# Layer 1 attention of a two-layer kernel: residual, last bias and attention's sum added by DVE instead of by identity products on PE, with a new planning order

## The chip, the cores and the metric

The kernel runs on one core of a Trainium2 chip. Five engines work in parallel, each through its own queue in order: PE (matrix products, with a separate weight-load row PEld), DVE (vector), ACT (scalar and activation functions), POOL (which here issues the scatters) and SP (which issues most of the loads). The metric is the device time of one execution in microseconds (us), given as the median of several runs. A profile is one further execution; it has its own time.

## The reference, cut to what matters

Two layers, each an attention part and a mixture-of-experts part, on eight batches of 512 tokens with 128 channels. The change lies in layer 1's attention:

```
x  = x + o.reshape(Bb, Tt, HEADS * DV) @ Wo
h2 = _ln(x, ln_w, ln_b)
return x + jax.nn.gelu(h2 @ W1 + b1, approximate=False) @ W2 + b2
```

This is applied to `_layernorm(x)` of the stream, and the stream itself is added outside: `x = x + _L1_attn_ref(_layernorm(x), ...)`. So four things meet in the stream that the router of layer 1's experts then reads: the stream before the attention, the attention's sum (with its own residual), the output of the GELU part, and the bias `b2`. `o` comes from a gated linear recurrence over the tokens, which the kernel runs as a scan.

## The kernel before, in words

The tokens of a batch lie as a tile of 128 partitions x 4 x 128 (one PSUM bank). Each batch is one "block". Layer 0's attention and experts come first and end near 440 us. Then the stage around the change begins: for each of the eight blocks a coroutine `attend(b)` and, behind it, `route1(b, px)`. After that stage the routed rows are read back expert by expert (`fetch`, `first`, `second`, lines 1698 to 1775), and the results are gathered and added (line 1825).

The order within the stage is not written by hand. Each coroutine yields the engine that it needs next and a cost, and a planner (`Order.run`) picks, of all the blocks' next steps, the one that can start first by those costs; ties and ranks are settled by the lists TURN, TURN_REST and TURN_ROUTE, one number for each block. What the planner picks becomes the fixed order of every engine's queue. A changed cost or rank therefore changes the order of all five queues.

The steps of a block that matter below:

- line 1162: `ys`, layer 0's expert results, is loaded; line 1174: PE adds the stream `x_b` and both halves of `ys` into a PSUM tile `px` by products with the identity; lines 1148 and 1149: DVE takes the moments.
- lines 450 and 456: ACT normalises `px` into `hn`; PE transposes it (line 440), and products with the weights follow (1234, 1250, 1263, 1275), with ACT functions behind them.
- line 1190, `residual()`: ACT copies `px` into `x_b`, gives the PSUM tile back, and normalises `x_b` into `u`, the attention's input.
- lines 1241 and 1299: ACT's queue writes keys, queries and decays to DRAM; line 1223: SP reads them back spread over the partitions as `kb`, `gb_both`, `qb_both`, 1 MB each.
- lines 1306, 1313, 1317: DVE's product, scan and product over 128 x 2048 elements. Line 1327: PE sums the result. Lines 1344, 1349, 456, 1337, 1355: the gated root-mean-square norm.
- lines 1360 and 1362: PE adds `u` (identity) and the product with `Wo` into a PSUM tile `pu`; moments, normalisation, transposes, line 1394 (W1), line 1398 (GELU, into `mT`).
- line 1377, `keep_sum()`: ACT copies `pu` back into `u`.
- line 1405: PE adds `x_b`, the bias `b2` and `u` into a new PSUM tile with three identity products of 128 x 512; line 1409: eight products with W2 go on top. `b2` lies on all partitions.
- `route1`: moments, normalisation, transposes, router product (1445), the eight best and their numbers on DVE (1457 to 1464), counts (1485 to 1489), their sums over the partitions on PE (1493, 1494), the target rows `si` (1502), ACT's copies of the row and its weight into one of six `rows` buffers (1552, 1553), and for each of 128 pairs of token tile and choice one scatter on POOL (line 1540). Each group of four scatters has a numbering instruction before it (1535). The expert stage can begin only when all 128 have landed.

The four PSUM tiles named `acc` (line 1085) are shared by 1174, 1327, 1360 and 1405.

Of the kernel before, what the change touches and what calls it, by code (L numbers as in the profile page):

```python
# [63 lines left out]
PE, DVE, ACT, POOL, SP = "PE", "DVE", "ACT", "POOL", "SP"  # L64
# [125 lines left out]
def two_layers(ctx: ExitStack, tc: tile.TileContext, a: dict, out: bass.AP):  # L190
    nc = tc.nc
# [9 lines left out]
    def ring(pool, n, shape, name, dtype=F32):  # L201
        return Ring([pool.tile(shape, dtype, tag=f"{name}{i}", bufs=1, name=f"{name}{i}") for i in range(n)])
# [6 lines left out]
    def load(name, shape, src, queue=nc.gpsimd, pool=const):  # L209
        t = pool.tile(shape, F32, name=name)  # L210
        queue.dma_start(t, src)
        return t

    xs = []
    for b in range(B):
        x_b = keep.tile([P, NT, C], F32, tag="x", name=f"x_{b}")
# [8 lines left out]
    ident = const.tile([P, P], F32, name="ident")  # L225
# [68 lines left out]
    tokens, columns = [P, NT, C], [P, S]  # L294
# [60 lines left out]
    b2 = load("b2", [P, C], a["L1_attn_b2"].partition_broadcast(P))  # L355
# [6 lines left out]
    order = Order()  # L362
# [79 lines left out]
    def tiled(t2):  # L442
        return t2.rearrange("p (t c) -> p t c", t=NT)

    def chunk(t2, t):
        return t2[:, t * P : (t + 1) * P]

    def affine(dst, src, rs, sh):
        for t in range(NT):
            nc.scalar.activation(  # L450
                dst[:, t, :], src[:, t, :], AF.Identity, bias=sh[:, t : t + 1], scale=rs[:, t : t + 1]
            )
# [6 lines left out]
    def landing(us):  # L459
        s = Signal()  # L460
        s.set(order.later(us))
        return s
# [595 lines left out]
    u_ring = ring(work, 4, tokens, "u")  # L1058
# [26 lines left out]
    acc_ring = ring(stage_psum, 4, columns, "acc")  # L1085
    FLIGHT = 5

    TURN = [-56.5, 2.5, 31.0, 55.5, 10.0, 34.5, 86.0, 12.5]
    TURN_REST = [-12.5, -2.5, -24.0, 28.5, -84.0, 41.5, 163.0, 24.5]
    TURN_ROUTE = [-34.0, -91.5, -74.0, 17.0, -71.0, 58.5, 11.5, 42.5]  # L1090

    class Small:

# [41 lines left out]
    order = Order()  # L1135
# [21 lines left out]
    def attend(b):  # L1157

        x_b = xs[b]
# [9 lines left out]
        m = yield flight  # L1169
        yield landed  # L1170
        px = yield acc_ring
# [13 lines left out]
        u = yield u_ring  # L1185
        have_u = Signal()

        def residual():
            yield ACT, 0.6
            nc.scalar.copy(x_b, tiled(px))  # L1190
            acc_ring.give(order.now, px)
            yield ACT, 1.65
            affine(u, x_b, m.rs["u"][:, 0, :], m.sh["u"][:, 0, :])
            have_u.set(order.now)

        hn = yield hn_ring
        yield ACT, 1.65
        affine(hn, tiled(px), m.rs["u"][:, 1, :], m.sh["u"][:, 1, :])
        order.add(TURN[b], residual())
        ps = yield bank_ring  # L1200
        yield PE, 0.65
# [10 lines left out]
        def used_hT():  # L1212
            uses[0] -= 1
            if uses[0] == 0:
                h1_ring.give(order.now, hT)
# [15 lines left out]
        def keys_queries():  # L1231
# [11 lines left out]
            yield landing(LANDING)  # L1243
            order.add(TURN[b], spread_rows(pairs[b][:ng], kb_ring, have_kb, Signal()))
            order.add(TURN[b], spread_rows(pairs[b][ng:], qb_ring, have_qb, Signal(), gb_issued))

# [26 lines left out]
        ps = yield bank_ring  # L1273
        yield PE, 0.98
        nc.tensor.matmul(ps[:ng, :], lhsT=gkw, rhs=hT, start=True, stop=True)
        used_hT()
        order.add(TURN[b], keys_queries())
        order.add(TURN[b], values())
        order.add(TURN[b], gating())

# [9 lines left out]
        ps = yield bank_ring  # L1290
# [29 lines left out]
        if finished[0] == B:  # L1320
            all_scanned.set(order.now)
        yield Rank(TURN_REST[b])

# [21 lines left out]
        squared.set(order.now)  # L1345
        order.add(TURN_REST[b], gated())
        ps = yield bank_ring
# [10 lines left out]
        pu = yield acc_ring  # L1358
        yield PE, 2.1
        nc.tensor.matmul(tiled(pu), lhsT=ident, rhs=u, start=True, stop=False)  # L1360
        for t in range(NT):
            nc.tensor.matmul(chunk(pu, t), lhsT=chunk(yT, t), rhs=wo1, start=False, stop=t == NT - 1)
        y_ring.give(order.now, yT)
        yield DVE, 1.5
        moments(m, tiled(pu), "m")
        yield ACT, 0.4, EXP
# [6 lines left out]
        have_sum = Signal()  # L1373

        def keep_sum():
            yield ACT, 0.6
            nc.scalar.copy(u, tiled(pu))
            acc_ring.give(order.now, pu)
            have_sum.set(order.now)

        order.add(TURN_REST[b], keep_sum())
        ps = yield bank_ring
        yield PE, 0.65
# [16 lines left out]

        yield have_sum
        ps = yield acc_ring
        yield PE, 5.0
        for part in (x_b, b2.unsqueeze(1).to_broadcast(tokens), u):
            nc.tensor.matmul(tiled(ps), lhsT=ident, rhs=part, start=part is x_b, stop=False)
        for t in range(NT):
            out_t = chunk(ps, t)
            for c in range(2):
                nc.tensor.matmul(
                    out_t,  # L1410
                    lhsT=mT[:, c, t * P : (t + 1) * P],
                    rhs=w2[:, c, :],
                    start=False,
                    stop=t == NT - 1 and c == 1,
                )
        m_ring.give(order.now, mT)
        u_ring.give(order.now, u)
        flight.give(order.now, m)
        order.add(TURN_ROUTE[b], route1(b, ps))

    def route1(b, px):
# [59 lines left out]

        order.add(TURN_ROUTE[b], shares())

# [45 lines left out]

        order.add(TURN_ROUTE[b], biases())  # L1530
        sent = [Signal() for _ in range(NT)]
# [17 lines left out]
        for t in range(NT):  # L1549
# [3 lines left out]
            nc.scalar.copy(rw[:, :, WEIGHT], m.ex[:, t, :])  # L1553
            order.add(TURN_ROUTE[b], scatter(t, rw))
        xr_ring.give(order.now, xr)
# [308 lines left out]
```

## Time and profile before

| what | value |
|---|---|
| median of 3 runs (lowest, highest) | 994.44 us (993.44, 996.89) |
| the profiled execution's own time | 989.84 us |
| its span, first to last instruction | 988.1 us |
| mean granted PE clock | 0.865 |
| PE busy | 786.4 us (80%) |
| DVE busy | 615.4 us (62%) |
| ACT busy | 490.4 us (50%) |
| POOL busy | 447.9 us (45%) |
| line 1405, three forms, 16 matmul rows each | 10.1, 10.0 and 9.0 us busy |
| line 1190, ACT copy of `px` | 8 times, median 596 ns |
| line 1377, ACT copy of `pu` | 8 times, median 620 ns |
| line 1540, scatters on POOL | 128 times, median 964 ns, 556.6 to 757.7 us |

Busy time is how long an engine's instructions ran; its share of the span is a mean over stages with different limits. A product of 128 x 512 in fp32 stands as two matmul rows in the profile, so eight products are 16 rows. The rows of pipelined products overlap, so what a product costs the engine is the distance from its start to the next one's start, not its duration. The granted clock says what part of full speed PE had.

### The profile page before, as it was taken

Reading aid. Unit: us, or ns where it says so; the run is one execution under the profiler, and the core shown is the slowest. Engines: PE = TensorE matmul, PEld = TensorE weight load, DVE = VectorE, ACT = ScalarE, POOL = GpSimd, SP = SyncE. Lnnn points to the kernel's source line nnn. Section 1 sums busy time; section 2 is a strip of 40 time slices with the busy share of each in tenths; the row PEclk is TensorE's granted clock in tenths of the full one; section 3 lists DMA queues with packets and bytes.
Section 4 is the critical chain, followed back from the end, with each engine's and each line's share of the span. In section 5 each row is a group of like instructions: output and inputs, shape, how many; then the busy total and the mean of one; then the engine's idle time right before and its main releaser. Section 6 shows DMA issues by size and latency. Waiting matters only on the chain. (4 is left out here: it accounts for less than half of the span.)

```text
span 988.1 us, 12411 instructions
## 1 busy us (share of the span) xinstructions
PE 786.4 (80%) x3523; PEld 487.0 (49%) x3523; DVE 615.4 (62%) x1599; ACT 490.4 (50%) x1072; POOL 447.9 (45%) x469
## 2 busy tenths in 40 slices
PE   5988899899598889977779999969755999888500
PEld 3634466455254544433224544435432999778500
DVE  5579998879769411112478568686442787666408
ACT  5644665565253403435766988756620555444200
POOL 7200002330845361550000378587775577777750
PEclk9888889799977889998898998979757999999955
DMA  7897674739324503004995067777112544332139
GB/s 174 213 261 160 162 187 107 197 96 215 79 71 109 164 8 86 23 22 148 221 238 137 33 153 203 172 182 212 52 49 66 129 126 116 108 104 81 54 115 348
DMA packets 75527, 132.91 MB, mean 135 GB/s; under 512 B 12819, under 2 KB 54673, under 8 KB 67265
## 3 DMA queue, kind: packets, MB, share of 16 engines
q1 hardware_dynamic: 46400, 91.12, 36.6%
q0 software_dynamic: 14832, 28.88, 9.8%
q10 hardware_dynamic: 14224, 12.11, 4.3%
q8 instruction: 28, 0.46, 0.2%
q14 instruction: 43, 0.34, 0.1%
HBM read 94.79 MB, written 41.14 MB: 138 GB/s over the span
## 5 line engine op out<-in xcount | busy, mean ns | idle before, releaser
L1540 POOL DMA_INDIRECT rows<-rows,si x128 | 148.9, 1164 | 159.6 <-issue 140.9
L880 POOL DMA_INDIRECT row<-rows,si x64 | 90.6, 1415 | 211.3 <-DVE qT L591 109.1
L1775 POOL DMA_INDIRECT res<-qy,to x144 | 139.9, 971 | 57.8 <-issue 29.2
L1744 ACT ACTIVATE qh<-mid,qw 128x128 f32<-128x128 f32 x288 | 79.7, 377 | 116.8 <-PE mid L1738 81.5
L675 PE MATMUL acc<-add,center 128*128 128x512 f32 x128 | 78.6, 770 | 17.3 <-DVE add L704 14.7
L1738 PE MATMUL mid<-dT,qw 128*128 128x128 f32 x576 | 74.7, 282 | 15.9 <-DVE dT L1728 15.9
L1738 PEld LDWEIGHTS mid<-dT,qw 128*128 128x128 f32 x576 | 68.9, 195 | 21.1 <-DVE dT L1728 21.0
L1756 PE MATMUL qyp<-qw,qh 128*128 128x128 f32 x576 | 71.7, 277 | 0.0
L698 DVE TENSOR_TENSOR_SCAN add<-dec,add 128x2048 f32<-128x2048 f32 x16 | 70.8, 4424 | 0.7
L1756 PEld LDWEIGHTS qyp<-qw,qh 128*128 128x128 f32 x576 | 68.3, 194 | 0.0
L179 ACT ACT_TABLE_LOAD x48 | 61.6, 1283 | 5.8 <-issue 3.2
L675 PEld LDWEIGHTS acc<-add,center 128*128 128x128 f32 x128 | 30.7, 251 | 62.4 <-issue 35.3
L1016 POOL DMA_INDIRECT res<-y,de x32 | 31.5, 984 | 43.3 <-DVE y L1010 35.7
L1712 DVE COPY qw<-fw 128x258 f32 x144 | 45.7, 317 | 8.5 <-ACT qh L1744 1.4
L666 ACT ACTIVATE dec<-dec 128x2048 f32<-128x2048 f32 x16 | 30.5, 1908 | 30.0 <-DVE dec L686 30.0
L1327 PE MATMUL acc<-kb,ident 128*128 128x512 f32 x64 | 36.1, 716 | 10.1 <-DVE kb L1317 10.1
L1713 DVE COPY qw<-fw 128x256 f32 x144 | 43.1, 300 | 0.2 <-issue 0.2
L793 PE MATMUL bank<-xT,rw 128*128 128x512 f32 x64 | 38.5, 733 | 5.3 <-ACT xT L785 3.6
L1148 DVE BATCH_NORM_STATS2 st<-acc 128x6 f32<-128x128 f32 x64 | 17.4, 272 | 33.9 <-PE acc L1174 32.4
L1825 DVE TENSOR_TENSOR x<-x,yk 128x512 f32<-128x512 f32 x32 | 21.5, 690 | 25.5 <-DMA yk<-res 24.6
L692 DVE TENSOR_TENSOR add<-add,vT 128x2048 f32<-128x2048 f32 x16 | 36.7, 2292 | 0.5
L686 DVE TENSOR_TENSOR dec<-add,kT 128x2048 f32<-128x2048 f32 x16 | 36.6, 2287 | 0.3
(349 smaller groups left out, 1698.0 us busy)
## 6 DMA issues: line engine op xcount, KB each, us to landing
add<-keys SPq DMA_DIRECT2D x16, 1024.0 KB
qb_first<-queries SPq DMA_DIRECT2D x8, 1024.0 KB
qb_second<-queries SPq DMA_DIRECT2D x8, 1024.0 KB
kb<-pairs SPq DMA_DIRECT2D x8, 1024.0 KB
gb_both<-decays SPq DMA_DIRECT2D x8, 1024.0 KB
qb_both<-pairs SPq DMA_DIRECT2D x8, 1024.0 KB
yk<-res SPq DMA_DIRECT2D x8, 1024.0 KB
de<-rows SPq DMA_DIRECT2D x108, 65.0 KB
```

The costliest lines, as they stand in the source:

```text
L179: self.load(table)
L675: nc.tensor.matmul(acc, lhsT=center, rhs=st[:, j, :], start=g + j == 0, stop=(g + 1) * J + j == D + J - 1)
L698: nc.vector.tensor_tensor_scan(flat, dec.rearrange("p j t -> p (j t)"), flat, 0.0, ALU.mult, ALU.add)
L793: nc.tensor.matmul(ps, lhsT=rw1[:, c * P : (c + 1) * P], rhs=xT2, start=True, stop=True)
L880: nc.gpsimd.indirect_dma_start(out=row0_w[(b * NT + t) * 2 + k], out_offset=bass.IndirectOffsetOnAxis(ap=m.si[:, t, k : k + 1], axis=0), i ...
L1540: nc.gpsimd.indirect_dma_start(out=rows1_w[(b * NT + t) * K1 + k], out_offset=bass.IndirectOffsetOnAxis(ap=m.si[:, t, k : k + 1], axis=0), ...
L1712: nc.vector.tensor_copy(w1_q[:, i, :], fw1[:, bass.ds(at, WE)])
L1713: nc.vector.tensor_copy(w2_q[:, i, :], fw2[:, bass.ds(at, I1)])
L1738: nc.tensor.matmul(mid[c][:, here], lhsT=w1_q[:, i, c * P : (c + 1) * P], rhs=dT[:, here], start=True, stop=True)
L1744: nc.scalar.activation(hT[:, c, here], mid[c][:, here], AF.Gelu, bias=w1_q[:, i, I1 + c : I1 + c + 1])
L1756: nc.tensor.matmul(ps[:, here], lhsT=hT[:, c, here], rhs=w2_q[:, i, c * C : (c + 1) * C], start=c == 0, stop=c == NC1 - 1,)
L1775: nc.gpsimd.indirect_dma_start(out=res1_w[4 * q + i], out_offset=bass.IndirectOffsetOnAxis(ap=to[:, i : i + 1], axis=0), in_=y[:, i, :], i ...
```

## The change

In `residual()` DVE now forms `px + b2` into `x_b` (one addition of 128 x 512, out of PSUM), and ACT normalises `u` directly out of PSUM; the PSUM tile is given back after that. In `keep_sum()` DVE adds `pu` to `x_b` in place. So `x_b` now holds stream, bias and attention's sum before the last step, and line 1405 has one identity product where it had three. `u` is free again right after line 1362. The planner is told costs of 0.68 us for each addition and 3.2 us for the shorter product step in place of 5.0 us, and the three lists of ranks are new. Line numbers of the changed kernel are one higher than those of the kernel before from line 1190 to 1362, two higher from 1363 to 1400, one higher at 1405 and 1409, and equal from 1420 on.

```diff
-    TURN = [-56.5, 2.5, 31.0, 55.5, 10.0, 34.5, 86.0, 12.5]
-    TURN_REST = [-12.5, -2.5, -24.0, 28.5, -84.0, 41.5, 163.0, 24.5]
-    TURN_ROUTE = [-34.0, -91.5, -74.0, 17.0, -71.0, 58.5, 11.5, 42.5]
+    TURN = [-95.0, 25.0, 52.0, 57.5, -0.5, 61.0, 138.5, 6.0]
+    TURN_REST = [-21.5, 23.5, -5.5, 9.5, -138.5, 49.5, 129.5, -3.5]
+    TURN_ROUTE = [-3.5, -148.5, -160.5, 20.0, -176.5, 65.0, 4.0, 43.0]
...
         def residual():
-            yield ACT, 0.6
-            nc.scalar.copy(x_b, tiled(px))
+
+            yield DVE, 0.68
+            nc.vector.tensor_add(x_b, tiled(px), b2.unsqueeze(1).to_broadcast(tokens))
+            yield ACT, 1.65
+            affine(u, tiled(px), m.rs["u"][:, 0, :], m.sh["u"][:, 0, :])
             acc_ring.give(order.now, px)
-            yield ACT, 1.65
-            affine(u, x_b, m.rs["u"][:, 0, :], m.sh["u"][:, 0, :])
             have_u.set(order.now)
...
         y_ring.give(order.now, yT)
+        u_ring.give(order.now, u)
         yield DVE, 1.5
         moments(m, tiled(pu), "m")
...
         def keep_sum():
-            yield ACT, 0.6
-            nc.scalar.copy(u, tiled(pu))
+            yield DVE, 0.68
+            nc.vector.tensor_add(x_b, tiled(pu), x_b)
             acc_ring.give(order.now, pu)
...
-        yield PE, 5.0
-        for part in (x_b, b2.unsqueeze(1).to_broadcast(tokens), u):
-            nc.tensor.matmul(tiled(ps), lhsT=ident, rhs=part, start=part is x_b, stop=False)
+        yield PE, 3.2
+        nc.tensor.matmul(tiled(ps), lhsT=ident, rhs=x_b, start=True, stop=False)
...
         m_ring.give(order.now, mT)
-        u_ring.give(order.now, u)
         flight.give(order.now, m)
```

## The prediction

> **What bounds the kernel now.** I read the chain that ended last first. It goes back from the result additions through the expert stage to the last scatter of layer 1's routing, and stops there:
>
> ```profile
> 755.44 0.96 POOL rows L1540
> 756.39 0.30 issue
> 756.70 2.29 DMA rows<-rows,si
> 759.58 2.05 DMA de<-rows
> ```
>
> Columns: start, duration, what. The expert stage waits for the 128th scatter (ends 757.66), so the change is worth what it moves that scatter. POOL's own order of time shows what sets it (columns: start, duration, engine, line, ..., idle before and what ended it):
>
> ```profile
> 556.57 0.97 POOL L1540 DMA_INDIRECT rows<-rows,si  x1 [112.83 <-issue]
> ...
> 561.33 0.16 POOL L1535 IOTA rows<- 128x4 int32 x1
> 561.77 0.97 POOL L1540 DMA_INDIRECT rows<-rows,si  x1 [0.28 <-ACT xr L450]
> ...
> 596.50 4.76 POOL L1540 DMA_INDIRECT rows<-rows,si  x1 [0.30 <-issue]
> ...
> 627.81 0.96 POOL L1540 DMA_INDIRECT rows<-rows,si  x1 [0.31 <-issue]
> ...
> 641.93 0.97 POOL L1540 DMA_INDIRECT rows<-rows,si  x1 [9.21 <-ACT rows L1553]
> ...
> 756.70 0.96 POOL L1540 DMA_INDIRECT rows<-rows,si  x1 [0.30 <-issue]
> ```
>
> A group of four scatters takes 5.22 us (561.77 less 556.57, and the same between most groups), so 32 groups take 167.0. The scatters' busy sum is 148.9 us; at 0.964 each it would be 123.4, so some are stretched: 25 us in all. The one break is 9.2 us at 632.7. Check: 556.6 + 167.0 + 25 + 9.2 = 757.8; the page has 757.7. So POOL is the bound from 556.6 on, whatever PE's share of busy time is, and the time is set by four terms: **first scatter, 167, stretching, breaks**.
>
> The stretched ones coincide with DVE's big operations:
>
> ```profile
> 596.07 4.42 DVE L1313 TENSOR_TENSOR_SCAN kb<-gb_both,kb 128x2048 f32<-128x2048 f32 x1
> ...
> 627.71 0.75 DVE L1337 SCALAR_TENSOR_TENSOR yT<-acc,rmsw,gate 128x512 f32<-128x512 f32 x1 [3.36 <-ACT sq L1344]
> ```
>
> The scan at 596.07 holds the scatter of 596.50 until about its own end. The operation at 627.71, which has one operand in PSUM, lies over the scatter of 627.81 and leaves it at 0.96.
>
> Before the first scatter PE is the full engine, by the table of stretches (columns after the length: PE, PEld, DVE, ACT, POOL busy, granted clock, DMA share, GB/s):
>
> ```profile
> 500.00:520.00 20.00, 13.28 (x35) 4.69 (x34) 17.81 (x21) 12.76 (x26) 0.00 (x0) 0.99 0.98 238
> 520.00:540.00 20.00, 19.16 (x59) 9.94 (x59) 16.97 (x27) 11.20 (x22) 0.00 (x0) 0.83 0.58 126
> 540.00:560.00 20.00, 19.59 (x82) 11.04 (x81) 11.89 (x59) 18.94 (x45) 2.82 (x3) 1.00 0.09 34
> ```
>
> Until about 520 it is the DMA (share 0.98) and then DVE (17.8 of 20) that lead; from 520 PE does.
>
> **The change part by part.**
>
> *Removed from PE.* PE's order of time gives the distance from start to start:
>
> ```profile
> 533.00 1.02 PE L1405 MATMUL acc<-b,ident 128*128 128x512 f32 x2
> 533.86 1.02 PE L1405 MATMUL acc<-u,ident 128*128 128x512 f32 x2
> ```
>
> 0.86 us each, two of them in eight blocks: 13.7 us of PE work. *Removed from ACT:* eight copies of 0.596 and eight of 0.620, 9.7 us; two more table loads stand in the new order (2 x 1.28), so 7.2 net. *Added to DVE:* 16 additions. No row is exactly this form; the nearest are line 1269 with one PSUM operand (679 ns) and line 1355 without (682 ns), so 0.68, 10.9 us in all. By line 1337, which has three operands (738 ns), it would be 11.8. None of these three sums is the result: none lies on POOL. They count only through the four terms.
>
> *First scatter.* Here the new order decides. I read the order in which the changed kernel's instructions stand on each engine. Before, the first block's router product stands behind 68.3 us of PE work from the stage's start, and its scatters go out 20 us ahead of the second block's. In the new order two blocks are brought to the router together: both router products stand behind the fourth block's sum (line 1327), at 78.6 and 79.5 us of PE work, and DVE looks up both blocks before it forms the first target rows. So what PE saves is spent on more work ahead of the first scatter. I followed the three queues from the second scan, which waits for its load at 501.1 in both orders. DVE then runs without a break: 4.35 scan, 0.6 gate, 2.2 product, 0.6 new addition, 2.2 product, 1.65 moments, 0.6 new addition, 0.85 shift and gate, 4.35 scan, 0.6, 0.6 new addition, 2.2 product: 521.9, and 522.9 with a wait for ACT's square at 514. Before, the third block's product ended at 522.0: the three new additions cost what the other order saves. From there PE has 26.8 us until the first of the two router products ends (before: 23.4, of which one slow sum took 5.8 for 3.4): 523.1 + 26.8 = 549.9. Along it ACT's inputs arrive in time by my walk, two of them by less than 0.6 us. Then moments of the third block until 551.0, look-up and counts 4.0, shares 0.75, second look-up 4.0, target rows 1.15: 560.9, scatter at 561.3. The bare sum of PE work gives a later end: the count product stands at 84.8 us of PE work for 72.6 before, so 550.3 + 12.2 = 562.5 for it and some 564.5 for the scatter. I take 562, nearer to the walk, because part of PE's idle time is filled: +5.4.
>
> *Breaks.* The fifth block's keys leave ACT's queue much earlier in the new order: before, SP could issue its load at 567.6, and the scan came at 596; by my walk the keys now leave at 539 and the scan comes near 566. The third routed block then needs its count product 34.5 us of PE work behind the second's. Before, 35.8 us took 42.2, so near 600; POOL, busy with two blocks (41.8 and 14 of stretching), asks for it at 617. For the later ones the margin grows (by PE work 132 against 614 and a demand near 638, 148 against 636 and 663). No break: -9.2. ACT may stand still for one of the six row buffers, but then POOL has five groups, 26 us, in hand.
>
> *Stretching.* Four blocks' product, scan and product lie behind the first scatter in both orders. Before, three of the four stretched POOL by 6.8 each and the one that met the break by 4.5; without the break all four cost 6.8: 27.2, +2.2. Do the new additions stretch scatters too? Eight of them lie behind the first scatter. A scatter is stretched by what is left of the DVE operation, some 0.6: bounds 0 and +5. The Trainium skill, page "GPSIMD Engine Reference" (the table at its head), says that POOL shares its SBUF interfaces with VectorE and contends with instructions in a two-port mode or with two SBUF inputs. Both additions have one input in PSUM. Read as "DVE work delays POOL" the rule speaks against the change and makes the sum below +3.4; read with its condition it makes it -1.6, and the line at 627.71 agrees. I take 0.
>
> *Other moved steps.* The seventh load of `ys` on SP now stands behind the first block's three loads instead of between them: the decays come up to 2 us earlier, the second block's keys as before. The third block's decays leave ACT some 12 us later than before (behind the square of line 1344), so SP's `gb` load waits and the key loads behind it; by bytes the DMA engines have work until 504, so the loads still land by 516 and 529, where DVE's order asks for them at 515 and 528: 0 to +1.5, inside my 562. The PSUM tile `px` is held through the 1.65 us of normalising; its next user waits for that in no step of my walk. The 32 weight loads behind the last scan come sooner and are waited for by nobody before 757.
>
> **Sum.** 5.4 - 9.2 + 2.2 = -1.6 us on the 128th scatter; what follows it is unchanged. Against the profiled execution: span 988.1 to 986.5, its time 989.8 to 988.2. That execution lies 4.6 below the median of 994.44, so for the median I carry the difference over: 992.8. This kernel's measurement can tell about 0.3%, 3 us, from no change, so the likeliest case sits inside it.
>
> **Rivals.**
>
> *The first scatter stays where it was, 556.6.* For: PE loses 1.7 us in each block ahead of it and ACT two copies, and the walk has ACT waits at 513 to 518 that a slightly earlier load would shorten. Against: two look-ups and the fourth block's sum now stand ahead of it. Then -9.2 + 2.2 = -7.0: 987.4.
>
> *The first scatter comes at 568 or later (slower).* One mechanism: PE's granted clock between 523 and 550. Before, PE stood idle for 3.0 us until 519.65, and the next sum ran slow:
>
> ```profile
> 522.01 5.96 PE L1327 MATMUL acc<-kb,ident 128*128 128x512 f32 x8 [0.84 <-DVE kb L1317]
> ```
>
> That is 2.4 us over the 3.43 at full clock. My walk leaves PE idle for 2.2 and 1.3 us near 502 and 508 and not longer behind; if a wait stretches into such a pause and 6 us of the 26.8 run at half speed, the first scatter is at 568 and the sum +4.4: 998.8. It decides from a first scatter at 563.6 (no gain) and 566.6 (slower by 0.3%).
>
> *POOL runs dry anyway, or the additions do stretch scatters.* A break of 9 us, as before at 641.93, gives +7.6: 1002; the additions' upper bound gives +3.4: 997.8. Against: margins of 17 us and more; the line at 627.71.
>
> *The change doesn't do what it says.* PE loses its 13.7 us, but nothing that POOL waits for: that is close to my likeliest case.
>
> **How the numbers follow.** Likeliest (first scatter 560 to 565.5, own range 991 to 996.5): 0.42. First scatter as before or earlier: 0.24. Late first scatter: 0.20. Break or stretching: 0.14. Faster than 991.5: the second case whole and 0.12 of the first, 0.36. Slower than 997.4: all of the third but 0.04, and 0.14: 0.30, and 0.02 of the first, 0.32. Same: the rest, 0.32. The range leaves out a tenth at each end, below the second case's value by the 2 us that loads could gain, and above the third's but short of the break's: 985.4 to 1001.
>
> **What would show it.** First scatter at 560 to 564; no idle of POOL over 1 us between the scatters; stretching of 25 to 29 us; additions at 0.65 to 0.74; scatters under a new addition at 0.96; PE's stage work 13.7 shorter. Wrong if the first scatter is outside 557 to 567, if POOL waits for ACT's rows, or if something behind the last scatter moves.

## The result, and the profile after

The changed kernel is slower: 1002.71 us median of 14 runs (992.16 to 1010.43) against 994.41 us for the kernel before (14 runs, 990.43 to 1000.48). The ratio is 1.0073, 95% interval [1.0045, 1.0101]. The forecast was 992.8 us, "within 0.3%", with a range up to 1001.

The profiled execution of the changed kernel took 992.16 us (span 990.5), the lowest of the 14. So the two spans, 988.1 and 990.5, differ by less than the medians do, and I compare the stage around the change instead of spans. The stage is counted from its first moments instruction (DVE's BATCH_NORM_STATS2 out of the first `px`), at 452.12 us in the execution before and 448.45 after, to the last instruction of the execution. Ahead of that moment both traces have the same instructions on each engine, and it moves between executions of one kernel (448.45, 459.15 and 458.93 in three of the changed one). Below, "+76.3" means 76.3 us after that moment.

The chain that ended last still goes through the last scatter on POOL, 3 us later by the clock of the span:

```profile
758.41 0.95 POOL rows L1540
759.37 0.30 issue
759.67 2.28 DMA rows<-rows,si
...
762.55 2.80 DMA de<-rows
```

POOL's order of time after the change (start, duration, engine, line, operation, idle before and what ended it):

```profile
563.65 0.96 POOL L1540 DMA_INDIRECT rows<-rows,si  x1 [124.14 <-ACT rows L1553]
...
571.99 4.64 POOL L1540 DMA_INDIRECT rows<-rows,si  x1 [0.30 <-issue]
...
617.64 0.15 POOL L1535 IOTA rows<- 128x4 int32 x1
621.07 2.39 POOL L1540 DMA_INDIRECT rows<-rows,si  x1 [3.29 <-issue]
...
673.27 0.97 POOL L1540 DMA_INDIRECT rows<-rows,si  x1 [1.19 <-issue]
...
759.67 0.96 POOL L1540 DMA_INDIRECT rows<-rows,si  x1 [0.30 <-issue]
```

The first scatter is at +115.2 (before: +104.5). The long break of 9.21 us (POOL standing idle between two scatters) is gone; two short ones, 3.29 and 1.19, are new. DVE in the same stretch:

```profile
563.65 0.69 DVE L1379 TENSOR_TENSOR x<-acc,x 128x512 f32<-128x512 f32 x1
...
571.43 4.42 DVE L1314 TENSOR_TENSOR_SCAN kb<-gb_both,kb 128x2048 f32<-128x2048 f32 x1
```

The new addition of 563.65 lies over the first scatter and leaves it at 0.96; the scan of 571.43 stretches the scatter of 571.99 to 4.64, as before. The stretches before the first scatter (length, then PE, PEld, DVE, ACT, POOL busy, granted clock, DMA share, GB/s):

```profile
500.00:520.00 20.00, 15.32 (x50) 6.64 (x48) 17.42 (x22) 14.85 (x33) 0.00 (x0) 1.00 0.90 212
520.00:540.00 20.00, 17.30 (x64) 9.17 (x65) 14.50 (x26) 13.82 (x24) 0.00 (x0) 1.00 0.62 154
540.00:560.00 20.00, 16.85 (x72) 9.04 (x71) 12.80 (x71) 15.67 (x39) 0.00 (x0) 1.00 0.65 150
```

PE is no longer the full engine from 520 on (17.3 and 16.9 of 20 for 19.2 and 19.6 before), and its clock was full. The sum of line 1328 that ran slow before runs at full speed here, and the identity product behind it stands once:

```profile
520.41 3.70 PE L1328 MATMUL acc<-kb,ident 128*128 128x512 f32 x8 [0.78 <-DVE kb L1318]
523.95 1.02 PE L1406 MATMUL acc<-x,ident 128*128 128x512 f32 x2
```

Nobody is full, so somebody waits. The four terms of the forecast, from two executions of the kernel before and three of the changed one (all that were profiled where the kernel before takes 990 to 1000 us):

| term | before | after | measured | forecast |
|---|---|---|---|---|
| first scatter | +104.5, +103.7 | +115.2, +114.4, +114.9 | +10.7 | +5.4 |
| POOL's breaks over 0.6 us | 9.2, 9.2 | 4.5, 3.3, 7.3 | -4.2 | -9.2 |
| stretching (scatters beyond 0.96 us each) | 25.4, 24.3 | 26.4, 28.0, 21.9 | +0.6 | +2.2 |
| first scatter to end of last | 201.1, 199.8 | 197.0, 197.9, 195.4 | -3.7 | -7.0 |
| behind the last scatter | 230.4, 229.0 | 229.8, 229.9, 228.9 | -0.2 | 0 |
| stage start to end | 536.0, 532.5 | 542.0, 542.1, 539.2 | +6.9 | -1.6 |

The 6.9 us agree with the 7.3 us that the ratio makes of 994.4. So the question is where the first scatter lost 5.3 us more than forecast, and where 5.0 us of the break stayed.

### The profile page after: what moved, and what is told of

Its sections match the earlier page's. It is cut to its first block, busy times and chain, and to the rows that moved or that the text cites. A ratio compares the mean times of both kernels' runs of the same rounds, so it can differ in the third digit from the quotient of the medians.

```text
span 990.5 us, 12341 instructions
## 1 busy us (share of the span) xinstructions
PE 773.6 (78%) x3491; PEld 487.6 (49%) x3491; DVE 626.8 (63%) x1615; ACT 483.7 (49%) x1058; POOL 447.1 (45%) x469
## 5 line engine op out<-in xcount | busy, mean ns | idle before, releaser
L880 POOL DMA_INDIRECT row<-rows,si x64 | 89.7, 1402 | 207.1 <-DVE qT L591 104.5
L1010 DVE TENSOR_TENSOR y<-yp,de 128x512 f32<-128x512 f32 x8 | 5.5, 692 | 49.5 <-PE yp L1009 49.5
L1328 PE MATMUL acc<-kb,ident 128*128 128x512 f32 x64 | 31.3, 635 | 6.0 <-DVE kb L1318 5.6
```

What stands on the lines that cost most here:

```text
L880: nc.gpsimd.indirect_dma_start(out=row0_w[(b * NT + t) * 2 + k], out_offset=bass.IndirectOffsetOnAxis(ap=m.si[:, t, k : k + 1], axis=0), i ...
```

## The experiments

Two kinds of experiments change the order. In the first the planner is given other arithmetic or other ranks and plans anew. In the second the planner's picks for one kernel are written out as a list, and another arithmetic follows the same list step by step; every edit has as many steps as the original, so the lists fit. "Exact order" below means the second kind. The orders of SP and POOL are then identical, DVE's too but for the additions; on PE and ACT PSUM tiles are exchanged among each other, and a few neighbouring steps change places where such a tile comes free at another time.

### Both kernels once more, the arithmetic in the old plan, PE's work given back

`a2_after_again` and `b2_before_again` are unchanged. In `p1` the changed arithmetic keeps the costs and ranks of before (the three lists and the costs are reverted, the additions stay). In `c1` the changed kernel gets PE's saving back as work, two products of the identity with zeros in each block:

```diff
         nc.tensor.matmul(tiled(ps), lhsT=ident, rhs=x_b, start=True, stop=False)
+        for _ in range(2):
+            nc.tensor.matmul(ps, lhsT=ident, rhs=zeros, start=False, stop=False)
```

> The changed kernel once more, for a second traced execution: its first one took 992.2 us though the median of its executions is 1002.7. Theory A (the first scatter decides): where the execution takes 1000 us or more, the first scatter is at 568 or later and POOL's stretching and breaks stay near 27 and 4.5 us. Theory B (breaks decide): the first scatter stays at 562 to 565 and POOL's idle time between scatters grows from 4.5 to 10 us or more. Theory D (elsewhere): the stage before 440 us or the expert stage behind the last scatter is longer and the scatters lie as in the first trace.

> The kernel before once more, for a second traced execution: the first took 989.8 us, the median is 994.4. Theory A: the first scatter 556 to 561, break 5 to 10 us. Theory D: the same 3 to 5 us are found outside the scatter stage.

> The change's arithmetic (two DVE additions, one identity product, u read from PSUM) with the costs and ranks of the kernel before given to the planner, so that nearly the old order stands. Theory A (the new order's late first scatter costs the time, the arithmetic itself gains): first scatter 553 to 557, time 3 to 8 us below the kernel before, ratio 0.992 to 0.997. Theory C (the additions themselves cost: DVE waits or stretched scatters): not faster than the kernel before, ratio 1.000 to 1.006.

> The changed kernel with two further identity products of a zero tile in each block at line 1406, so that PE has the 13.7 us back that the change took from it, in the new order. Theory A: the first scatter comes 2 to 4 us later than in the changed kernel (two blocks' products lie ahead of it), and the time is 2 to 5 us above it, ratio to the kernel before 1.009 to 1.013. Theory B (breaks behind, from ACT's rows and chains late on PE): more than 6 us above the changed kernel, with longer breaks. PE's work without effect: within 1 us of the changed kernel.

Measured: the two repetitions are in the table above (one run each: 1002.92 and 988.76 us). The two traced executions of the changed kernel, 992.16 and 1002.92 us, differ by 10.7 us, and this lies ahead of the stage (start at 448.45 and 459.15), where both have the same instructions: theory D. `p1` 1003.08 us, ratio 1.010 [1.0066, 1.0134]: first scatter +110.4, breaks 16.2 us. `c1` 1003.4 us, ratio 1.0126 [1.005, 1.0201]; its trace has the first scatter at +114.4, breaks of 5.6, and 541.9 us from the stage's start to its end, as the changed kernel has. So the 13.7 us of PE work that the change removed are worth nothing at this place in the new order: PE's work does not set the first scatter, though my walk from 523 to 550 had it so. And in the old plan the arithmetic by itself is no gain but a loss of 1%.

`p1` shows one reason. ACT's order of time, its `u` for three blocks:

```profile
477.87 1.51 ACT L450 ACTIVATE u<-acc,sh_u,rs_u 128x128 f32<-128x128 f32 x4 [1.51 <-DVE x L1190]
...
498.12 1.51 ACT L450 ACTIVATE u<-acc,sh_u,rs_u 128x128 f32<-128x128 f32 x4 [5.94 <-DVE x L1190]
...
508.36 1.51 ACT L450 ACTIVATE u<-acc,sh_u,rs_u 128x128 f32<-128x128 f32 x4 [1.21 <-DVE x L1190]
```

`u` reads the same PSUM tile as DVE's addition, only reads it, and still stands behind it: it waits for a semaphore that DVE raises. In `s1` (below), where `u` comes first, the addition waits for `u` (1.1 to 5.4 us, four times). Whether the chip needs this order or only the program's synchronisation sets it, no run here shows. Where the addition in turn stands behind a scan of 4.4 us, ACT stands too (5.94 us), and all that is queued behind `u`. Before, `u` read `x_b`, which ACT itself had copied. In the changed kernel's own order a wait of over 0.5 us is there once:

```profile
504.60 0.46 ACT L450 ACTIVATE u<-acc,sh_u,rs_u 128x128 f32<-128x128 f32 x1 [2.78 <-DVE x L1191]
504.67 0.33 ACTq L1242 DMA_DIRECT2D pairs<-kq  x1
```

I took this wait for the cause of the late scatter (theory W) and the order by itself, or the additions' own length, as rivals (O and, from here on, A).

### Halves of the change, and the order of `u` and the addition, planned anew

`o1`: the old arithmetic with the new lists of ranks. `s1`: `u` ahead of the addition. `h1`: only the last sum is DVE's. `h2`: only the residual is. All with the new ranks.

```diff
 s1 against the changed kernel
-            yield DVE, 0.68
-            nc.vector.tensor_add(x_b, tiled(px), b2.unsqueeze(1).to_broadcast(tokens))
             yield ACT, 1.65
             affine(u, tiled(px), m.rs["u"][:, 0, :], m.sh["u"][:, 0, :])
+            yield DVE, 0.68
+            nc.vector.tensor_add(x_b, tiled(px), b2.unsqueeze(1).to_broadcast(tokens))
 h1 against the changed kernel (residual() as before), and:
-        nc.tensor.matmul(tiled(ps), lhsT=ident, rhs=x_b, start=True, stop=False)
+        for part in (x_b, b2.unsqueeze(1).to_broadcast(tokens)):
+            nc.tensor.matmul(tiled(ps), lhsT=ident, rhs=part, start=part is x_b, stop=False)
 h2 against the changed kernel (keep_sum() as before), and:
-        nc.tensor.matmul(tiled(ps), lhsT=ident, rhs=x_b, start=True, stop=False)
+        for part in (x_b, u):
+            nc.tensor.matmul(tiled(ps), lhsT=ident, rhs=part, start=part is x_b, stop=False)
```

> The arithmetic of before in the new order (the three lists of due times alone are changed). All places from the first BN_STATS of the stage on. In the changed kernel the fourth scan starts at +81 and the first scatter at +114.4 to +115.2; before, +76 and +104.5. Theory W (ACT's u of the fourth block stands behind DVE's addition, which stands behind a scan, and the writes of pairs and decays stand behind u): here u reads x_b, which ACT itself copied, so the wait is gone: fourth scan near +77, first scatter near +110 (the two look-ups of the new order still cost 5), stage's start to end 537 to 539, ratio to before 1.002 to 1.004. Theory O (the new order is at fault by itself): fourth scan +81, first scatter +114 to +115, stage 541 to 543, ratio 1.007 or more. Theory A (the additions' own 0.68 us in DVE's run of scans): fourth scan +78, first scatter +111 to +112.

> The changed kernel with ACT's u ahead of DVE's addition, so that u waits for nothing of DVE's and the addition waits for u; all arithmetic of the change stays. Theory W: the idle of 3.5 us of ACT ahead of u is gone, pairs of the next block are written 3 us earlier, fourth scan near +77, first scatter near +110, stage 537 to 539, ratio to before 1.002 to 1.004. It may come out worse than that where DVE now waits for u: up to +2. Theory O and theory A: nothing moves, first scatter +114 to +115, ratio 1.007.

> Half of the change in the new order: the residual is copied by ACT as before and b2 stays a product with the identity; only the last sum is added by DVE out of PSUM. Theory W: no wait of u for DVE, fourth scan near +77, first scatter near +110, ratio 1.002 to 1.004. Theory O: first scatter +114 to +115, ratio 1.007. Theory A: in between, as half of the additions remain: +112.

> The other half in the new order: DVE adds residual and b2 out of PSUM and ACT's u reads the same PSUM tile; the last sum is copied by ACT and multiplied with the identity as before. Theory W: the wait of u stays, and with it all: fourth scan +80 to +82, first scatter +114 to +116, ratio 1.007 to 1.01. Theory O: the same. Theory A: in between: +112.

| run | ratio to before | first scatter | breaks | stage start to end |
|---|---|---|---|---|
| `o1` | 1.0244 [1.0185, 1.0304] | +118.0 | 22.6 | 561.0 |
| `s1` | 1.0165 [1.011, 1.0219] | +121.0 | 14.5 | 549.3 |
| `h1` | 0.9995 [0.9963, 1.0026] | +108.2 | 0 | 529.5 |
| `h2` | 1.0103 [1.004, 1.0165] | +119.3 | 10.7 | 550.1 |

`o1` and `s1` have no wait of `u` for DVE, and both are slower than before by more than the changed kernel is. That speaks against theory W in the new order. But these four decide neither W nor O: with other costs the planner makes another order each time, and the orders differ by more than the edits. `h1` is a case of it: it has no break at all and the earliest scatter of the new ranks, and is as fast as before. That is what the exact order is for.

### The same arithmetic in exactly the other's order

`xo` (and `xo2`, the same once more): the old arithmetic in exactly the changed kernel's order. `xa`: the changed arithmetic in exactly the order of before. `xs`: the last sum alone, in the order of before. `ysum`: the same in the new order. The edit to the planner's pick is the same in all:

```diff
+                if self.script is not None:
+                    if c[6] not in self.script:
+                        continue
+                    key = (self.script.index(c[6]),)
...
+            if self.script is not None:
+                del self.script[key[0]]
```

> The arithmetic of before (ACT's two copies, three identity products) with every step in exactly the sequence in which the changed kernel has it: what the planner picked there is written out as a list and followed. Theory P (place: in the new order the fourth block's decays stand behind the second block's sum and square, are written at +65.6 instead of +58.1, and the fourth scan and the first scatter follow; two look-ups come ahead of the first scatter): fourth scan +80 to +82, first scatter +114 to +116, fewer than 5 us of breaks; stage from its start to its end 541 to 545, ratio to before 1.007 to 1.012. Theory W (ACT's u waits for DVE's addition): here it waits for nothing, fourth scan +78, first scatter +111, ratio 1.003.

> The change's arithmetic (DVE's 16 additions out of PSUM, u normalised out of PSUM, one identity product) with every step in exactly the sequence of before. Theory P: decays written at +58 to +60 and fourth scan at +76 to +78 as before; first scatter +104 to +107; the break of 9 us stays or shrinks; ratio to before 0.998 to 1.004. Theory W: ACT idles 2 to 4 us ahead of u behind DVE's addition, pairs and decays are written later, fourth scan +79 or later, first scatter +108 or later, ratio 1.006 to 1.01, whatever the order.

> Half of the change in exactly the sequence of before: the last sum is added by DVE out of PSUM (one identity product less in each block); residual and b2 as before. If the additions cost nothing where they stand: first scatter +102 to +104, the break of 9 us as before, ratio 0.997 to 1.000. If an addition by DVE delays the work behind it by its own length: first scatter +106, ratio 1.002 to 1.004.

> Half of the change in exactly the new order: the last sum is added by DVE out of PSUM; residual copied by ACT and b2 multiplied with the identity as before. If the wait of u for DVE's addition costs time by itself: first scatter +110 to +112 against the changed kernel's +114.4 to +115.2, ratio 1.001 to 1.005. If the new order sets it whatever the arithmetic (theory P): +114 to +116, ratio 1.006 to 1.010.

> The arithmetic of before in exactly the new order, once more. First scatter +117 as before in the run with the low clock (ACT's two copies and PE's two products more stand ahead of it than in the changed kernel). If the order alone costs the time and the arithmetic gains in it: ratio 1.012 to 1.022, with breaks of over 10 us. If the arithmetic costs the time: ratio 1.005 or less.

These runs were made in two sessions in which the kernel before took 1086 to 1090 us instead of 990 to 1000, so their ratios belong to those sessions (below). They missed what was expected: `xo` and `xo2` 0.9999 with breaks of 36 us each, where `xo` was to have 1.007 to 1.012 with fewer than 5; `ysum` 0.9893 for 1.006 to 1.010; `xs` kept the time, 0.997, but with breaks of 41.5 us for 9. `xa`, 1.0111, came near what theory W had. So what the order alone costs in time, where the kernel before takes 990 to 1000 us, was not measured. What lies ahead of the first scatter can be compared: `xs` has its first scatter at +103.5, as the kernel before has it elsewhere, and `d1` (below) at +114.4, as the changed kernel has it.

| first scatter | order of before | new order |
|---|---|---|
| old arithmetic | +104.5, +103.7 | +117.3, +119.7 |
| last sum by DVE | +103.5 | +116.3 |
| all of the change | +112.9 | +115.2, +114.4, +114.9 |

By the means the order alone costs 14.4 us at the first scatter; the arithmetic takes 3.7 of it back in the new order, and costs 8.8 in the old one. (One or two executions each; the two of the old arithmetic in the new order differ by 2.4.) In the new order taking the residual half away, and with it the wait of `u`, gains nothing (+116.3): there theory W is not the cause, and the order is.

In the old order the price is the residual half, not the last sum (+103.5). Two things come with that half. In `xa` ACT's `u` waits 6.11 us for DVE's addition, as in `p1`; but the fourth scan comes only 2.5 us later than in `xs` (+78.8 for +76.3). The other 6.9 us lie behind that scan, and there it is the PSUM tile. PE's sum of line 1360 for the fourth block needs a free `acc` tile. In `xs` ACT's copy has just given one back (the copy starts at +84.8 of the stage), and PE goes on:

```profile
555.04 0.60 ACT L1398 COPY x<-acc 128x512 f32<-128x512 f32 x1
556.23 1.02 PE L1568 MATMUL acc<-u,ident 128*128 128x512 f32 x2
```

In `xa` the same tile is held until `u` has been formed from it, at +104.6; PE stands idle for 2.63 us, takes later work first, and has the sum at +95.4 for +86.0, behind the addition that empties another tile:

```profile
560.46 2.38 PE L648 MATMUL bank<-ident,hn 128*128 128x128 f32 x8 [2.63 <-ACT hn L658]
561.79 0.66 DVE L1587 TENSOR_TENSOR x<-acc,x 128x512 f32<-128x512 f32 x1
565.04 1.02 PE L1569 MATMUL acc<-u,ident 128*128 128x512 f32 x2
574.21 1.52 ACT L658 ACTIVATE u<-acc,sh_u,rs_u 128x128 f32<-128x128 f32 x4
```

(Stage starts 470.22 and 469.65; line numbers are 208 or 209 higher. In `p1` that sum is at +95.8.) So in the old order more is lost to the tile that is held longer than to the wait of `u`. No run separates the two; this split is read from the traces.

### The writes that the loads wait for

What is it in the new order? The fourth scan is at +81.8, +80.9 and +81.4 after the change (before +76.3, +75.5), and it waits for its load. From that scan to the first scatter it is 33.4 us in all three executions of the changed kernel and 28.2 in both of the kernel before. So of the 10.7 us half, 5.5, is there at the scan, and 5.2 lie behind it, where the new order has the second look-up and the fourth block's sum ahead of the scatter. The orders of time of ACT's queue, SP's queue and DVE in the kernel before, cut to the fourth block's loads: ACT's queue writes keys and decays, SP loads them, DVE's scan follows the load.

```profile
504.92 0.33 ACTq L1241 DMA_DIRECT2D pairs<-kq  x1
510.20 0.45 ACTq L1299 DMA_DIRECT2D decays<-gk  x1
...
516.38 0.52 SPq L1223 DMA_DIRECT2D kb<-pairs  x1
518.43 0.51 SPq L1223 DMA_DIRECT2D gb_both<-decays  x1
...
528.28 0.06 DVE L1311 MEMSET gb_both<- 128x3 f32 x1 [1.85 <-DMA gb_both<-decays]
```

The same after the change:

```profile
513.13 0.45 ACTq L1300 DMA_DIRECT2D decays<-gk  x1
...
506.75 0.51 SPq L1224 DMA_DIRECT2D kb<-pairs  x1
522.16 0.51 SPq L1224 DMA_DIRECT2D gb_both<-decays  x1
...
530.13 0.06 DVE L1312 MEMSET gb_both<- 128x3 f32 x1 [5.16 <-DMA gb_both<-decays]
```

Counted from the stage's start the fourth block's decays are written at +64.7 for +58.1 before, its `gb` load goes out at +73.7 for +66.3, the scan comes at +81.8 for +76.3. In ACT's queue that write now stands behind the square (line 1345) of the second block, which waits for PE's sum, as the third block's stands behind the first's. DVE waits 5.16 us for the load.

The scanned blocks are 0, 4, 7 and 1, in this order. `d1` moves three steps of the changed kernel ahead of the second block's sum: the product, the exponential and the write for the fourth block's decays. `d2` moves the same three of the third block too, and the fourth's keys with their write ahead of `u`; the third block's gate product gives way. Arithmetic and the other steps stay in the new order. `d3` is `d2` with only the last sum by DVE.

```diff
 d1, in the list of picks of the changed kernel
+move: (block 1: product of gk and za, exponential, write of decays) to behind (block 1: exp and ln of za)
 d2
+move: (block 7: exp and ln of za, product, exponential, write of decays) to behind (block 7: write of pairs)
+move: (block 7: its gate) to ahead of (block 1: its gate)
+move: (block 1: keys' product, copy, write of pairs; exp and ln of za, product, exponential, write of decays) to behind (block 1: lines 1285 and 1286)
```

> The changed kernel in its own order, but for three steps: the fourth block's last product for the decays (gk and za with the identity), its exponential and its write are moved ahead of the second block's sum. Theory P: decays written near +56 instead of +65.6, gb load issued by +64 instead of +72.6, fourth scan near +77, first scatter +110 to +111, stage 537 to 539, ratio to before 1.002 to 1.004 (the two look-ups are left). Theory W or a bound elsewhere (PE's work behind the third scan): first scatter stays at +114 to +115, ratio 1.007.

> The changed kernel, all its arithmetic, with the decays of the third and of the fourth block and the keys of the fourth written to DRAM ahead of the squares (in ACT's queue the third's decays stand right behind its keys, the fourth's keys and decays ahead of u); the rest in the new order. Theory P (these writes set the loads and these the fourth scan): third block's gb load issued near +49 instead of +55.6, fourth block's near +66 instead of +72.6, third scan +62 to +63, fourth +76 to +77.5, first scatter +109 to +111 (the two look-ups stay), stage 536 to 538.5, ratio to before 1.001 to 1.005. Rival (the loads come earlier, but PE or DVE behind the third scan set the pace): fourth scan +77 but first scatter +113 or later, ratio 1.006 or more. If DVE's and not the load's time sets the fourth scan: +80 or later.

> The sum alone (as in the half run before) with the writes early as in d2: theory P and no wait of u for DVE together. First scatter +105 to +109, no break over 5 us, ratio to before 0.992 to 0.999. If the early writes are worth nothing: first scatter as in the exact new order with the sum alone.

> The changed kernel once more, beside the early writes on the same chip. Where the kernel before takes 990 to 1000 us: ratio 1.005 to 1.010, first scatter +114 to +115, as before. Where it takes over 1070 us (lower granted clock, PE's work is worth more): like the early decays of one block on such a chip, 0.983 to 0.992. If the first reading of slower holds on any chip: 1.005 to 1.010 there too.

> The changed kernel with the early writes once more. Theory P: fourth scan +76 to +77.5 and first scatter +109 to +111 on any chip; stage and time 3 to 5 us below the changed kernel on the same chip, so a ratio to before of 1.001 to 1.005 where before takes 990 to 1000 us. If POOL's other breaks take back what the earlier scatter gives: the same time as the changed kernel within 2 us.

`d1` missed: the decays were written at +57.2, 7.5 us earlier, and the fourth scan stayed at +81.0 and the first scatter at +114.4. The write of the keys had slipped from +56.2 (in the changed kernel) to +58.3, from just ahead of SP's `gb` and `qb` loads of the third block to just behind them, and SP's load of those keys went from +58.3 to +69.0. `d2` moved both, and did at the scatter about what was expected:

```profile
505.19 0.33 ACTq L1450 DMA_DIRECT2D pairs<-kq  x1
509.20 0.45 ACTq L1508 DMA_DIRECT2D decays<-gk  x1
...
516.69 0.51 SPq L1432 DMA_DIRECT2D kb<-pairs  x1
519.72 0.52 SPq L1432 DMA_DIRECT2D gb_both<-decays  x1
...
531.89 0.06 DVE L1520 MEMSET gb_both<- 128x3 f32 x1
```

(Its second run; stage start 454.03; line numbers are 208 higher.) DVE no longer waits for the load. Fourth scan +76.4 and +78.0 in the two runs, first scatter +110.1 and +111.7: the place of the writes is worth 3.9 us at the first scatter by the means (3.2 in the second run, beside the changed kernel), and 6.8 stay. `d3` against `ysum`, the same moves with the last sum alone, in one session, has the fourth scan at +77.7 for +82.4 and the first scatter at +112.6 for +116.3: 3.7 us again. Its own forecast, a scatter at +105 to +109 and no break over 5 us, was missed: the breaks are 20.8 us, one of them 9.4.

In time: side by side in one session the changed kernel took 1002.17 us, ratio 1.0088 [1.0042, 1.0134], and `d2` 998.61 us, ratio 1.0073 [1.004, 1.0106]. By the medians that is 3.6 us, by the traces 3.3 (stage 539.2 and 535.9), by the ratios 1.5, and the intervals overlap. That the scatter moves is shown; that the time follows is likely and no more. The ratio that I had expected, 1.001 to 1.005, was missed.

### Why 5 us of breaks stayed

This is read from the traces; no run tests it. Every profiled execution of the changed kernel has it (10.18, 9.99 and 9.98 us). ACT's order of time in its first profiled execution, and DVE's:

```profile
575.95 1.50 ACT L450 ACTIVATE hn<-acc,sh_m,rs_m 128x128 f32<-128x128 f32 x4 [0.31 <-DVE sh_m L1155]
587.63 0.62 ACT L1552 COPY rows<-xr 128x512 f32<-128x512 f32 x1 [10.18 <-DMA rows<-rows,si]
...
591.28 0.62 ACT L1345 ACTIVATE sq<-acc 128x512 f32<-128x512 f32 x1
```

```profile
591.93 0.75 DVE L1338 SCALAR_TENSOR_TENSOR yT<-acc,rmsw,gate 128x512 f32<-128x512 f32 x1 [10.93 <-ACT sq L1345]
...
617.21 0.42 DVE L1502 TENSOR_REDUCE si<-tmp 128x16 int32<-128x256 f32 x1
```

ACT wants a row buffer for the second routed block and stands 10.18 us until a scatter has emptied one; GELU, square and with them the third block's routing stand behind it in the queue, DVE idles 10.93 us, and the third block's target rows are formed at 617.21, when POOL has 0.4 us of work left. The break of 3.29 follows. The third execution has two more, 2.65 and 1.32 us near +226, at a numbering instruction that waits for the landing of earlier scatters. With two blocks routed 2.7 us apart (target rows at +113.8 and +116.5; before +99.4 and +122.8), eight groups ask for six buffers at once. In the kernel before ACT never waits so between 555 and 760; in `h1`, whose two blocks stand 12.0 us apart, it waits 3.05 us there and POOL has no break. That more buffers would close the break was not tried.

### Where the kernel before takes 1086 to 1090 us

Eight runs fell in such sessions: `xo` 0.9999 [0.9965, 1.0032], `xo2` 0.9999 [0.9971, 1.0028], `xa` 1.0111 [1.0054, 1.0169], `xs` 0.997 [0.9933, 1.0006], `ysum` 0.9893 [0.9825, 0.9962], `d1` 0.9838 [0.9785, 0.9891], `d2` 0.986 [0.9818, 0.9902], `d3` 0.9909 [0.9878, 0.9941]. The same `d2` is 1.4% faster than before there and 0.7% slower elsewhere. In the recorded expectations I took this for a matter of the chip. The record does not bear that out: its chip number 2 stands for 1089.76 us of the kernel before in one session and for 993.64 us in a later one.

The expert stage behind the last scatter takes 275 to 283 us there for 229 to 230, and POOL's breaks grow (`d2` 18.5 us for 6.8; `xs` in the old order 41.5). The 100 us of `d2` that begin 4 us behind the last scatter, in the slower session and in the other (columns as above):

```profile
793.00:893.00 100.00, 83.97 (x574) 73.44 (x575) 58.94 (x214) 33.11 (x120) 50.06 (x52) 0.90 0.34 89
```

```profile
765.00:865.00 100.00, 94.81 (x795) 93.24 (x796) 76.58 (x266) 48.93 (x176) 69.01 (x72) 0.94 0.47 119
```

The granted clock, 0.90 for 0.94, is too small a difference for 28% fewer products (574 for 795), and every engine and the DMA are less busy. What grows is PE's idle time. From the last scatter to the end, PE's weight loads of line 1738 (columns: busy time, mean ns of one, then the idle time before and what ended it), in the slower session and in the other:

```profile
L1947 PEld LDWEIGHTS mid<-dT,qw 128*128 128x128 f32 x576 | 79.0, 214 | 38.6 <-issue 34.8 <-DVE dT L1937 3.8
```

```profile
L1947 PEld LDWEIGHTS mid<-dT,qw 128*128 128x128 f32 x576 | 70.0, 198 | 18.0 <-DVE dT L1937 17.9
```

"issue" is idle time in which the profile shows nothing that the engine waits for. Added up over all weight loads behind the last scatter (idle times of over 0.3 us), it is 55.6 to 62.0 us in the eight traces of these sessions, in some 50 pieces, and 3.1 to 18.9 us in the twelve others, in one or two. That is about as much as the expert stage is longer. Ahead of the first scatter, from the stage's start, it is 11 to 17 us in both kinds, so the first scatters could be compared. What makes PE stand so is open. So is whether the changed kernel itself gains there; `d1`, which is the changed kernel but for three steps and has its first scatter, does, and in the same session the old arithmetic in the changed kernel's order (`xo`) does not.

## Why the prediction was wrong

**The frame held.** POOL is the bound from the first scatter on, the work behind the last scatter did not change (-0.2), and the terms add up to the measured time (10.7 - 4.2 + 0.6 = 7.1 for 7.3 us). The additions cost what was read from line 1269: 0.69 and 0.68 us median on the two lines for 0.68. The first profiled execution looks like a hit by luck: it took 992.16 us for my 992.8 and has its first scatter at 563.65, inside the 560 to 564 that I gave as a sign, but its stage began 3.7 us earlier than in the execution before, and 10.7 earlier than in the second of its own kernel, which took 1002.92.

**The first scatter, +10.7 for +5.4: the step that failed is "Other moved steps".** It said that the third block's decays leave ACT some 12 us later, but "the loads still land by 516 and 529, where DVE's order asks for them". The delay was seen (8 to 10 us, and 6.5 to 7.5 for the fourth block's) and its price set at 0 to +1.5; the fourth scan came 5.5 us later. In the time of the execution before, the fourth load let the scan start at 533.9 (81.8 behind 452.1), not by 529. I had counted bytes; what counts here is that the program issues a load only when the write that it reads back has landed, and the write came late. `d2` sized the term: 3.9 us. Without it the first scatter is at +6.8 over before for my +5.4, so the walk's other part, two look-ups and the fourth block's sum ahead of the scatter, was nearly right in size (5.2 us behind the scan). Its reason was not: I made it a run of PE work, and `c1` shows that two more products per block do not move it. Which of those steps makes the 5.2 us was not tested.

**"The PSUM tile `px` ... its next user waits for that in no step of my walk"** left out the second reader: `u` waits for DVE's addition, 2.78 us once. In the new order that is no part of the loss (`ysum`). In the old order, which I did not walk, the next user does wait as well: the held tile comes with 6.9 us of `xa`'s loss, the wait of `u` with 2.5.

**Breaks, -4.2 for -9.2.** The step that failed is the clause "ACT may stand still for one of the six row buffers, but then POOL has five groups, 26 us, in hand". ACT did stand, 10.18 us; by the trace POOL used up its groups while the third block's routing stood in ACT's queue, and ran dry for 3.3 us in each of the three executions. I put the third block's count product near 600 in the time of the execution before; it came at 614.97, which is 618.6 in that time.

**Stretching, +0.6 for +2.2, and the additions' part of it, 0: right.** Scatters under a new addition stay at 0.96, as the rule of the Trainium skill (page "GPSIMD Engine Reference", the table at its head) has it when it is read with its condition; here the line at 563.65 shows it.

**The rivals.** "First scatter at 568 or later" gave 998.8, and the scatter came where it would be 567.3 in the time of the execution before. Its mechanism, PE's clock, did not act: the clock was 1.00 from 500 to 560. "POOL runs dry" was the sign of the second loss. "The change doesn't do what it says", for PE loses "nothing that POOL waits for", was true of PE's 13.7 us.

**Open:** `h1` is 3 to 6.5 us shorter than before in the stage by its trace, and its ratio, 0.9995, shows nothing of it; `d2` is 1.7 us longer than before in the stage by its second trace, and 0.4% to 1.1% slower. One or two executions of each are too few to tell whether the part ahead of the stage differs. No version was found that beats both kernels where the kernel before takes 990 to 1000 us; `h1` beats the changed one.

## What to carry to other kernels

Where a planner makes the order, compare an arithmetic change in both exact orders: here the order cost some 14 us at the first scatter, and the arithmetic gave back 4 or cost 9, depending on the order. When a load reads back what another queue has written, follow the write, its place in the writing engine's queue and the loads that it lands behind, not the bytes. And moving a copy from ACT to DVE leaves a wait between them if both still read the same PSUM tile, and holds that tile until the second has read it: ask who needs the next one.

## What was not expected of the hardware

- Two engines that only read one PSUM tile went one behind the other; where ACT had to wait for DVE's addition it was 0.8 to 6.1 us (`p1`, `xa`, the changed kernel), by what DVE had in its queue.
- A write of 256 KB that was issued 0.7 us ahead of two loads of 1 MB let the load that depends on it go out 2.1 us after it (504.67, 506.75 in the changed kernel); issued behind them it took 10.7 us (`d1`: +58.3, +69.0) and 11.5 us (before: 504.92, 516.38). The place ahead of the loads is not all: one that was issued 2.3 us ahead of two such loads, but 7.6 us behind the last of the loads before, took 8.5 us (the changed kernel: +34.1, +42.6).
- The same kernel was 0.7% slower than the kernel before in one session and 1.4% faster in another, where PE stood for some 50 us more without a cause that the profile shows.
